# First 512 queries in four parts, the product of the decay factors in the lead-in, and the last combination in two steps

## The chip, the cores and the metric

The kernel runs on one core of one Trainium2 chip. The time is that of one execution on the device, in microseconds (us); several runs are made and their median is given. A core has five engines that each work through their own queue of instructions in order: TensorE (PE in the profile, with its weight loads as PEld), VectorE (DVE), ScalarE (ACT), GpSimd (POOL) and SyncE (SP, which here only starts transfers). They wait for one another by semaphores. Transfers between the chip's memory (HBM) and the on-chip buffer (SBUF) are made by 16 DMA engines. Results of TensorE land in PSUM, eight banks of 128 x 512 numbers.

## The reference

Two layers are computed on x of 2 sequences of 1024 tokens, 256 numbers each. Layer 0 is an attention with 16 query heads and 8 key heads of 16 numbers, whose output gates a feed-forward network with weights looked up from 16 values. Layer 1 is a recurrence whose output gates a mixture of 8 experts (two per token) with shared experts. Cut to what matters:

```python
# layer 0, attention
scores = jnp.einsum('bsdkg,btdk->bkgst', q, k) / jnp.sqrt(jnp.float32(E))
w = jax.nn.softmax(scores, axis=-1)
ctx = jnp.einsum('bkgst,btdk->bkgsd', w, v)          # then ctx @ W_O.T
# layer 0, feed-forward: w = lut[idx] for each of three weight matrices
h = jax.nn.silu(gate) * up
# layer 1, recurrence over t, for each head of 64 numbers
w = sigmoid(xn @ Wx @ Ww + bw)
state = (1.0 - w_t)[..., :, None] * state + k_t[..., :, None] * v_t[..., None, :]
y_t = jnp.einsum('bhi,bhij->bhj', r_t, state)        # then y @ Wout
# layer 1, experts
out = jax.nn.silu(g_sh) * u_sh @ shared_down.T
out = out + jnp.einsum('neh,ne->nh', y, combine)     # two experts per token
```

Each half of a layer is normalized first, and the feed-forward result goes through a SiLU, is multiplied by the attention's (or recurrence's) result and added to x.

## The kernel before

**The order.** All work is cut into steps. A step is a Python function that issues a few instructions on several engines, and has a letter. The string ORDER (lines 78 to 100, 1962 letters) says in which order the steps are issued; `go` takes letter after letter and calls that letter's next step. Nothing is reordered later: an engine gets its instructions in the order of the letters. So a step that waits on one engine holds up all later steps' instructions on that engine.

**The attention.** Tokens lie in 16 tiles of 128. For each tile there are statistics (`a`), a normalized copy (`b`), transposes for a pair of tiles (`e`), the product with the q, k, v weights (`f`, 4 TensorE passes of 512 columns; VectorE multiplies by cosine and sine, L205), the rotation on GpSimd (`g`, L223 and L226), and the transposes of the keys of a pair of tiles (`h`). `j` and `l` (`turn_q`, L264) transpose the queries of half a sequence, 512 queries of four heads, once without and once with their row maxima. A group g is four heads of a sequence; it has 16 units. `m` (`largest`, L274) makes for 128 queries and 512 keys of one head the scores and their maximum on VectorE (L290); four heads use four groups of 32 rows of TensorE. With the maximum as 17th number of a query, `w` (`weigh`, L296) makes scores of 128 keys and 512 queries that have the maximum taken off (L303), and ScalarE takes the exponential (L307). `v` (`gather`, L310) multiplies the four heads' exponentials by the values, adding up over the eight key tiles in one bank (L318). The first `l` needs the maxima of all 512 queries of its group, 32 `m` steps. `y`, `p` and `q` divide, transpose and project. Meanwhile GpSimd decodes the feed-forward weights (`z`, L252 and L256), up to 491 us. The exponentials have 22 buffers (EB).

**The middle.** `A` are the steps of layer 0's feed-forward: `gate_up0` (L506, L488) and `down0` (L522). At `>` the attention's pools are closed. Then eight loads for layer 1 are issued on SyncE, each of which waits until the memory that it takes is free: w1, gb, bw, gate, msk, wds, wgs (L581 to L599) and last `fold` (L1005), which is Wx transposed beside Ww, 512 KB, held in the buffer of `rd`. `rec_setup` (L1010, the first `i`) multiplies the two (wxwp, L1019), so that the decay needs one product per token rather than two, copies the result to wxw and then clears `rd`. It stands behind the first letter after `>`, so that TensorE meets it after one `down0`. `n` normalizes for layer 1, `o` is the routing, `s` the shared experts' first part, `i` the inputs of the recurrence.

**The recurrence and the end.** The recurrence of a block of 512 tokens (`r`) has seven `level` steps (L1127; 32 TensorE passes, then on VectorE L1134, L1162 and L1168) with `fold_in` (`c`, L1173: levels 0 to 4 on VectorE, L1193, the last two on ScalarE), then transposes (`turn_k`), states, reads and two `result` steps, which write s_sb. F, X, G, H, D and S handle 39 tiles of routed tokens: indirect fetch, transposes, gate and up (L912), transposes, down (L937) and an indirect write of the rows to y_h. When all rows are written, `k` loads the two expert results of 128 tokens, `d` makes the shared experts' second part (L970), and `u` combines:

```python
for k in range(2):                                                    # L983
    nc.vector.scalar_tensor_tensor(g, yk[:, k, :], wts[:, k, t : t + 1], src, ALU.mult, ALU.add)
    src = g
nc.scalar.activation(g, g, AF.Silu)                                   # L988
nc.gpsimd.tensor_tensor(g, s_sb[:, t, :], g, ALU.mult)                # L989
nc.vector.tensor_tensor(g, g, xs[:, t, :], ALU.add)                   # L990
nc.sync.dma_start(out_d[ts(t, P), :], g)                              # L991
```

Of the kernel before, what the change touches and what calls it, by code (L numbers as in the profile page):

```python
# [18 lines left out]
P = 128  # L19
# [20 lines left out]
EB = 22  # L40
# [38 lines left out]
abzbaazbbeebabfgeffbggbfahegffbgbjfhggfmmmhghmmmmemmmjmzmzmmmmmmmmmmmmmfmzmmmmmzmfjzmmmmlmwwwwmm  # L79
mwwwmwzmmwzzwmwmwmzmwmwwwmmmwwwwmwmmmvwwmmvmwmwzzwmwvwmmmmwwvgzwwmmgmmmlavvmwmmmwzwbvvmwzmwmwmwm  # L80
wmwmwmwjbmwzwmmmzzwweyhwmmwmmwmvwmzmmvzwwmmfmwwmvwmwgmwwzmavwmmmmwwvvwmwlvazvwmmmmwwfmmwwwwmjzmm
mwwzmwwmwzwmmmwzwmwvmwgmmmwzwvmwmwmwwmwmwwmzmmmlyvwmmmvmwwmvwmzwmvbwzmmwvwzmmbwvwwmmwwmmhezwwmmj
mwwmbmmwwvwwmmvzmmwwwwmvmmwmwwwvmmmwwwlfyjwwbmzwvzmwzmwvwwzmmvmwwmvwwmmwmmwfmwwmeywwmmzzmwmwwwmz
mgwzzmmfmmmmzwmwvvwwmmzzwwvmmmwgwmvmwwmwmvwmmwvmmwgmlfwwwmzvwzwmmvwmwmzmmwwjywmmwwzmmwgwmmmzwzhw
mwwwmmzvwmwmwmmvvwwzwzmmmwvmwmwwmwvmmzwmjlvwzwzmwmmwvmwwwmmmzvhwwmwmzmwzzzzzwmmwmwwzmmwwmmwwmwmm
vwwzmwzmmvwzmwwmwmvwmmmwzwzwvylwwmmwmzvmmmwwwvmmmmwwwzvvzwmwzzmzmzwmwjmzwwmmwzwwywmwzwmwmmvmzzwm
zmppzjvzzmmzwwwwwvzmwwzwlvmwmmvwmwwmwvmmmwwwzmvvwmmwwmwzmqmmwwwwmmqwwmzmwmzzwmvmmwwvwwmmmmmvvmmm
wwzmpylwwmmwmvwmwwmmwvwzwwwwzmmzvwwwmmwzmvwmmmmwwwqpwmmwwmwzmzjwmmmmwmmpqmmwwvvwmmwjvmzwwmvpwwww
qzy<pzqlwzmwmvmwmwmwwvmwmmwmwvwmwmwmvmwmwmwmwqmwmwzwmwwmwmmwmmwmwpwmwmmwmvvwmmmwmmvwwwmvlywwzmvm
wwwmmwvmwmwwmAAmwwzmvmwwmvwwzmmmmwzmAyAmzmmmwwwmAjwmmwzwmmAwwmwmwmmlwwmvmwwwmmmvvmwwwwwwvmmmvwww  # L90
wmwvvwzmmmwmwzzvwwzmmwwmmjwmwmzmmwmvwwmwvwmmmAAwwwwvmwmmjvwmwmlwmwwmmvmmmmmmwvvmwwwAyAmmwmvwmwzw
wmmzwmmwwwwmmmwwmwwmwwmwyqwmmwmmwwvvmwmmmwwvwmzwwlvwmmmmwwvwmwvmwmmmwwvvmwmzwmwmwwmwwyzmmmwwmwmA
wwmmzmwzmvvwwwmmmwvmwmwzwwwvlwzwwzwvwwwwvwwwwvvwwwwwwwwAywwwwvvwwwAwwwwpvvvwwwwAwwwwqpAvvvqApypA
qpqAAAqpAqAApApqAAq>AinnAAniAAAinAoAAAsAAiAninAAiAoAAnoArrnnrsoAAAAinrinAoAocAcnrAAAAoAAoAiociA)
nriinnrcsnrsocsooirsoosocosooisooosooooscoooosooooroooiooooroiroooioooooooroo]rFrrrFXiXcFGXFGFrH
GXHciXDGDrFFHHXSicSGDXrFHFiGcXDSFSrcHDGDGXiXSHGFFHGDXSDFHSXFGHDFGXrHcXDGSFiFHrSScXDSGXHGFrDDXrSr
HGHFrXGFSDFrHXGXDHGDSrrFHGSDHFiXXSrDSFGXcDrSHGFFHiXDHcDGFXSSGXSDHGDHrHXGDFrHcScFGiFSrXFDXcDHFSGr
ScDXGHGXrHDHFcGSXSFrDHDSXGrSrGFXHSiFGFDSHrXDrrrDrHGXcDHGSXDFrSHSFXSGcDrHGDcXrHGcDSSrHDSSkkrkicrc
kcdduukukuukridkkurkurkudurkkukukdukdruuuu
# [3 lines left out]
def attention(nc, tc, st, b0, small, singles, xs, xnT, s_sb, wlut, ident, epst, wqkv_d, rope_d, lut_d, idx_d, wo_d):  # L103
# [169 lines left out]

    def largest(n, i):  # L274

        g, u = divmod(n, 16)
        b, T = divmod(g, NQT)
        c, half = divmod(u, 2)
        if (g, c) not in tops:
            tops[g, c] = att2.tile([P, 2, 4], F32, tag="top", name=f"top_{g}_{c}", bufs=4)  # L280
        at = slice(SLOT * i, SLOT * (i + 1))
        ps = bank(f"mx_{n}_{i}")
        nc.tensor.matmul(  # L283
            ps,
            qTs["qTa", g, c // BC][at, ts(c % BC, P)],
            kTs[b][at, T // 2, ts(half, 512)],
            start=True,
            stop=True,
        )
        nc.vector.tensor_reduce(tops[g, c][:, half, i : i + 1], ps, AX.X, ALU.max)  # L290
        done[g, c] = done.get((g, c), 0) + 1
        if done[g, c] == 8:
            top = tops.pop((g, c))
            nc.vector.tensor_tensor(qns[b][:, T, c, :, HD], top[:, 0, :], top[:, 1, :], ALU.max)

    def weigh(n, i):  # L296

        g, u = divmod(n, 16)
        b, T = divmod(g, NQT)
        h, c = divmod(u, 8)  # L300
        at = slice(SLOT * i, SLOT * (i + 1))
        ps = bank(f"sc_{n}_{i}")
        nc.tensor.matmul(  # L303
            ps, kTs[b][at, T // 2, ts(c, P)], qTs["qTb", g, h][at, :], start=True, stop=True
        )
        e = att2.tile([P, 512], F32, tag="e", name=f"e_{n}_{i}", bufs=EB)
        nc.scalar.activation(e, ps, AF.Exp, scale=1.0 / math.sqrt(E))  # L307
        es[n, i] = e

    def gather(n):  # L310

        g, u = divmod(n, 16)
        b, T = divmod(g, NQT)
        h, c = divmod(u, 8)
        if c == 0:
            cxs[g, h] = bank(f"cx_{g}_{h}")
        for i in range(4):
            nc.tensor.matmul(  # L318
                cxs[g, h][SLOT * i : SLOT * (i + 1), :],
                values(b, c, 4 * (T // 2) + i),  # L320
                es.pop((n, i)),
                start=(c == 0),
                stop=(c == CPB - 1),
            )
        if c == CPB - 1:
            ct = att2.tile([P, 512], F32, tag="ct", name=f"ct_{g}_{h}", bufs=1)
            nc.scalar.copy(ct, cxs.pop((g, h)))
            cts[g, h] = ct
# [36 lines left out]
    def each(f, *ranges):  # L365
# [10 lines left out]
        "l": each(turn_q, ["qTb"], range(GROUPS), range(2)),  # L376
# [11 lines left out]
def two_layer_kernel(  # L388
# [55 lines left out]
    s_sb = pers.tile([P, NTC, E], F32, name="s_sb")  # L444

# [112 lines left out]

    steps["<"] = [end_sequence0]
# [21 lines left out]
    nc.sync.dma_start(w1, w1_d)  # L581
    gb = moe.tile([P, 2, KC], F32, name="gb")
    nc.sync.dma_start(gb, gb_d)
    bw = moe.tile([P, KC], F32, name="bw")
    nc.sync.dma_start(bw, bw_d)
    gate = moe.tile([P, KC, SLOT], F32, name="gate")
    nc.sync.dma_start(gate, gate_d)
    msk = moe.tile([P, NLEV, HALF], I32, name="msk")
    nc.sync.dma_start(msk, msk_d)
    wds = moe.tile([P, NFS, E], F32, name="wds")  # L590
    nc.sync.dma_start(wds, wds_d)
# [7 lines left out]
    nc.sync.dma_start(wgs, wgs_d)  # L599
# [379 lines left out]
    def combine(t):  # L979

        yk, src = tiles.pop(("yk", t)), tiles.pop(("s", t))
        g = mt[0].tile([P, E], F32, tag="g", name=f"g1_{t}", bufs=3)
        for k in range(2):  # L983
            nc.vector.scalar_tensor_tensor(
                g, yk[:, k, :], wts[:, k, t : t + 1], src, ALU.mult, ALU.add
            )
            src = g
        nc.scalar.activation(g, g, AF.Silu)  # L988
        nc.gpsimd.tensor_tensor(g, s_sb[:, t, :], g, ALU.mult)  # L989
        nc.vector.tensor_tensor(g, g, xs[:, t, :], ALU.add)  # L990
        nc.sync.dma_start(out_d[ts(t, P), :], g)  # L991
# [7 lines left out]
    wxw = rec.tile([P, KC, E], F32, name="wxw")  # L999
# [3 lines left out]

    fold = rd.rearrange("p a r s -> p (a r s)").rearrange("p (k f d) -> p k f d", k=KC, d=E)
    nc.sync.dma_start(fold[:, :, 0:2, :], fold_d)  # L1005
# [4 lines left out]
    def rec_setup():  # L1010
# [4 lines left out]
        ps = bank1("wxwp")  # L1015
        psv = ps.rearrange("p (k d) -> p k d", k=KC)
        for kc in range(KC):
            for k in range(KC):
                nc.tensor.matmul(  # L1019
                    psv[:, kc, :],  # L1020
                    fold[:, k, 0, ts(kc, P)],
                    fold[:, k, 1, :],
                    start=(k == 0),
                    stop=(k == KC - 1),
                )
        nc.scalar.copy(wxw, psv)
# [282 lines left out]
    def each(f, *ranges):  # L1309
# [22 lines left out]
        "u": each(combine, range(NTC)),  # L1332
    }
# [126 lines left out]
```

## Time and profile before

| | us |
|---|---|
| median of 3 runs (1015.49 to 1016.59) | 1015.66 |
| the profiled execution | 1016.48 |
| its span, first to last instruction | 1014.7 |
| first product with the q, k, v weights starts (its weights land at 12.07) | 12.2 |
| first maximum on VectorE | 32.3 |
| first exponential | 57.4 |
| last exponential's scores | 543.6 |
| closing of the attention's pools, first load behind it | 577.8 |
| last indirect write issued | 953.2 |
| first and last instruction of the combinations on VectorE | 963.1, 1007.6 |

The mean granted TensorE clock over the span is 0.983 of full. The page's first part gives busy time, share of the span and number of instructions for each engine; in its second part the span is cut into 40 slices of 25 us, and each digit is the busy share of a slice in tenths. A float32 product of TensorE shows as two passes; "x12" in a chain or timeline counts passes. In the chain of waits, "issue" is time in which the engine waited for nothing that the profile shows. TensorE's passes are pipelined and their ends are modelled, so durations of single passes overlap.

### The profile page before, as it was taken

What the parts mean: (1) busy time and instruction counts of PE and PEld (TensorE: products, weight loads), DVE (VectorE), ACT (ScalarE), POOL (GpSimd) and SP (SyncE); (2) the same over time, 40 slices, a digit from 0 to 9 for tenths busy, and PEclk for the clock granted to TensorE, in tenths of its full rate; (3) what the DMA queues carried; (4) which work ended last, traced back from release to release, by engine and by line L of the source; (5) the groups of instructions that cost most, each with busy time, mean ns of one, the idle gap of its engine ahead of it and who ended that gap; (6) DMA issues with size and microseconds to landing.
All of it is one profiled execution on the core that took longest, in us unless ns stands there. A gap on an engine that the chain in (4) does not pass through costs nothing.

```text
span 1014.7 us, 16476 instructions
## 1 busy us (share of the span) xinstructions
PE 961.0 (95%) x6324; PEld 503.6 (50%) x6324; DVE 628.8 (62%) x1234; ACT 536.5 (53%) x1007; POOL 578.6 (57%) x475
## 2 busy tenths in 40 slices
PE   6999999999999999999999889999999998999882
PEld 3444333343433443334335454656476776677671
DVE  4889887877777686667620133578757433554753
ACT  3167756566665666677687235435324444453221
POOL 6999899999999999999301020202002453434121
PEclk9999999999999999999999979999999999999997
DMA  4000000000000000000000121015101121212133
GB/s 148 1 1 12 1 12 1 1 12 1 12 2 12 1 12 1 1 1 1 1 1 1 56 102 42 1 42 170 44 1 37 62 66 52 64 48 63 64 115 93
DMA packets 18086, 34.48 MB, mean 34 GB/s; under 512 B 2878, under 2 KB 11344, under 8 KB 17664
## 3 DMA queue, kind: packets, MB, share of 16 engines
q1 hardware_dynamic: 12855, 21.18, 6.6%
q0 software_dynamic: 3920, 10.74, 3.4%
q10 hardware_dynamic: 1232, 1.51, 0.4%
q8 instruction: 51, 0.84, 0.3%
q14 instruction: 28, 0.22, 0.1%
HBM read 22.01 MB, written 11.40 MB: 33 GB/s over the span
## 4 chain that ended last, share of the span: by engine, by line
PE 86%; DVE 4%; issue 4%; ACT 2%; POOL 1%; DMA 1%; another core or an unknown queue 1%; ACTq 0%; POOLq 0%; DVEq 0%
PE sc L303 15%; PE mx L283 14%; PE cx L318 12%; PE gu L506 6%; PE gue L912 4%; PE gus L676 4%; PE d L522 4%; PE dne L937 3%; PE qkv L200 3%; PE lev L1155 3%; PE so L360 1%; PE kp L1059 1%; DVE w L1193 1%; PE s L1278 1%; POOL g L989 1%
## 5 line engine op out<-in xcount | busy, mean ns | idle before, releaser
L290 DVE TENSOR_REDUCE top<-mx 128x1 f32<-128x512 f32 x512 | 324.5, 684 | 85.0 <-PE mx L283 57.3
L307 ACT ACTIVATE e<-sc 128x512 f32<-128x512 f32 x512 | 272.0, 604 | 125.0 <-PE sc L303 68.7
L283 PE MATMUL mx<-kT,qTa 32*128 32x512 f32 x1024 | 281.2, 627 | 0.5 <-DVE top L290 0.5
L303 PE MATMUL sc<-qTb,kT 32*128 32x512 f32 x1024 | 277.9, 624 | 0.8 <-ACT qTb L271 0.8
L252 POOL TENSOR_SCALAR pick<-idx,lut 128x544 f32<-128x544 int32 x120 | 252.4, 2103 | 11.2
L256 POOL TENSOR_TENSOR wlut<-wlut,pick 128x544 f32<-128x544 f32 x120 | 160.7, 1339 | 10.0
L303 PEld LDWEIGHTS sc<-qTb,kT 32*128 32x128 f32 x1024 | 98.2, 183 | 84.5 <-DVE top L290 28.0
L283 PEld LDWEIGHTS mx<-kT,qTa 32*128 32x128 f32 x1024 | 100.9, 183 | 77.2 <-DVE top L290 34.6
L318 PE MATMUL cx<-e,vpad 128*32 128x512 f32 x1024 | 131.6, 602 | 0.0
L889 POOL DMA_INDIRECT xg<-xn_h,who x39 | 38.9, 996 | 104.9 <-ACT s_sb L1285 69.7
L532 POOL TENSOR_TENSOR sgt<-s_sb,g 128x256 f32<-128x256 f32 x16 | 12.1, 756 | 141.2 <-ACT g L530 141.2
L950 POOL DMA_INDIRECT y_h<-ye,who x39 | 40.7, 1043 | 73.3 <-ACT ye L945 28.2
L506 PE MATMUL gu<-xnT,wlut 128*128 128x512 f32 x160 | 73.4, 597 | 0.0
L318 PEld LDWEIGHTS cx<-e,vpad 128*32 128x32 f32 x1024 | 22.6, 108 | 87.0 <-issue 75.3
L912 PE MATMUL gue<-wgu,xT 128*128 x156 | 53.3, 464 | 1.6 <-ACT hTe L930 0.8
L921 DVE TENSOR_TENSOR sge<-sge,gue 128x176 f32<-128x176 f32 x39 | 13.2, 337 | 59.8 <-ACT sge L920 55.3
L522 PE MATMUL d<-wlut,h 128*128 128x256 f32 x192 | 45.4, 389 | 1.1 <-DVE h L497 0.6
L506 PEld LDWEIGHTS gu<-xnT,wlut 128*128 128x128 f32 x160 | 29.1, 190 | 33.9 <-issue 28.1
L676 PE MATMUL gus<-xnT,wgs 128*128 128x512 f32 (+1 forms) x96 | 43.3, 597 | 0.0
L937 PE MATMUL dne<-wd,hTe 88*128 x156 | 40.8, 384 | 2.5 <-DVE w L1193 1.2
L516 DVE TENSOR_TENSOR h<-sg,gu 128x512 f32<-128x512 f32 x20 | 13.7, 687 | 46.0 <-ACT sg L515 24.6
L1162 DVE TENSOR_TENSOR rd<-rd,up 128x512 f32<-128x512 f32 x48 | 31.0, 687 | 17.6 <-PE xgTp L901 4.4
(219 smaller groups left out, 1283.9 us busy)
## 6 DMA issues: line engine op xcount, KB each, us to landing
xn_h<-xn SPq DMA_DIRECT2D x16, 256.0 KB, 2.7
yk<-y_h SPq DMA_DIRECT2D x16, 256.0 KB, 2.9
wgu<-in_wgu SPq DMA_DIRECT2D x1, 2816.0 KB, 11.3
idx<-in_idx SPq DMA_DIRECT2D x8, 272.0 KB, 2.8
out_x<-g SPq DMA_DIRECT2D x16, 128.0 KB, 1.7
wd<-in_wd SPq DMA_DIRECT2D x1, 1408.0 KB
w<-in_w SPq DMA_DIRECT2D x1, 1024.0 KB
wgs<-in_wgs SPq DMA_DIRECT2D x1, 704.0 KB, 6.2
```

The costliest lines, as they stand in the source:

```text
L252: nc.gpsimd.tensor_scalar(dst, codes[piece], float(j), lut[:, j : j + 1], ALU.is_equal, ALU.mult)
L256: nc.gpsimd.tensor_tensor(wlut[:, at], wlut[:, at], dst, ALU.add)
L283: nc.tensor.matmul(ps, qTs["qTa", g, c // BC][at, ts(c % BC, P)], kTs[b][at, T // 2, ts(half, 512)], start=True, stop=True,)
L290: nc.vector.tensor_reduce(tops[g, c][:, half, i : i + 1], ps, AX.X, ALU.max)
L303: nc.tensor.matmul(ps, kTs[b][at, T // 2, ts(c, P)], qTs["qTb", g, h][at, :], start=True, stop=True)
L307: nc.scalar.activation(e, ps, AF.Exp, scale=1.0 / math.sqrt(E))
L318: nc.tensor.matmul(cxs[g, h][SLOT * i : SLOT * (i + 1), :], values(b, c, 4 * (T // 2) + i), es.pop((n, i)), start=(c == 0), stop=(c == CPB ...
L506: nc.tensor.matmul(hT0[which], wlut[:, lo + kc * P :][:, 0:P], xnT[:, kc, ts(n, 512)], start=(kc == 0), stop=(kc == KC - 1),)
L522: nc.tensor.matmul(po[:, 0:E], hidden(n)[:, f, ts(k, P)], wd0[:, f, :], start=(f == 0), stop=(f == NF0 - 1),)
L676: nc.tensor.matmul(ps[:sz, which, :], wgs[:, kc, which * SH_CH + lo : which * SH_CH + lo + sz], xnT[:, kc, ts(n, 512)], start=(kc == 0), s ...
L912: nc.tensor.matmul(ps[:, 0 : 2 * EI], xT[:, kc, :], late["gu"][:, kc, bass.ds(e * (2 * EI), 2 * EI)], start=(kc == 0), stop=(kc == KC - 1),)
L937: nc.tensor.matmul(ps[:, 0:E], hT[:, k, :], late["d"][:, k, bass.ds(e * E, E)], start=(k == 0), stop=(k == 1),)
```

## The change

The kernel gets a new ORDER of 1982 letters with two new letters, `W` (once) and `U` (16 times), and three more `l`.

- **Queries in parts.** The first transposes of 512 queries with their maxima become four `turn_first` steps of 128 queries. For the first eight units a `weigh` makes four products of 128 queries by 128 keys side by side in a bank, for one part of the queries and four key tiles; `gather` takes them in 16 products of 128 columns. The first `l` now stands behind 14 `m`, before behind 36. By the 64th `m` both orders have 32 `w` and 4 `v`. Before the first `m` the new order has 9 `f`, 5 `e`, 3 `h` and 1 `j`; the old one 8, 4, 2 and 1. EB is 21; the most exponentials that the new order has open is 21, the old one 22.
- **Decay product.** `fold` is loaded on ScalarE's queue, behind the attention's first loads, into the first part of s_sb. The product is the step `W`, behind the first `l`. The other seven loads stay behind `>`, in another order. `rec_setup` keeps its other instructions, behind two `n` now. `>` stands behind 27 `A` rather than 26: the first `down0` of the second block is now issued ahead of it, directly behind the last `gate_up0` of that block and ahead of the last `project`.
- **Last combination.** `u` ends with the SiLU; the product on GpSimd, the addition (VectorE for even tiles, GpSimd for odd ones) and the write are `U`. At the last `S` the new order has issued 46 `r` and 22 `c`, the old one 49 and 25; at `]`, where the routing ends, 17 `r` against 13.

The two ends of the order and the code:

```diff
-EB = 22
+EB = 21
...
-abzbaazbbeebabfgeffbggbfahegffbgbjfhggfmmmhghmmmmemmmjmzmzmmmmmmmmmmmmmfmzmmmmmzmfjzmmmmlmwwwwmm
...
-ScDXGHGXrHDHFcGSXSFrDHDSXGrSrGFXHSiFGFDSHrXDrrrDrHGXcDHGSXDFrSHSFXSGcDrHGDcXrHGcDSSrHDSSkkrkicrc
-kcdduukukuukridkkurkurkudurkkukukdukdruuuu
+aaabbbabeazbebfgefgfgbzbbbfgehfgeffghgfjfhmmgmhmmgmmmmmmjfmmmlWmwmzmmwwwmmwlmmwmmwzmwwmwmmzwmmwm
...
+DHXrcSHDGXDGHFFXGHXSGDFXSrHcDFHGGSFXSXFrSDDHGSHDGSFSXDHrrHiGXSDDrFGXHrrSSrDrHSGDrHcDSSckrdkkuukU
+ukrdkUkucUurciUkkiuUUkurckduUrcdcurUkukUkuUrrUdukurUkrduUUuuUU
...
+    def turn_first(c):
+        if c == 0:
+            qTs["qTb", 0, 0] = att2.tile([P, 512], F32, tag="qTb", name="qTb_0_0")
+        ps = bank(f"qTbp_0_{c}_0")
+        nc.tensor.transpose(ps[:, 0:P], qns[0][:, 0, c], ident)
+        nc.scalar.copy(qTs["qTb", 0, 0][:, ts(c, P)], ps[:, 0:P])
...
     def weigh(n, i):
...
+        if n < 8:
+            for k in range(4):
+                nc.tensor.matmul(
+                    ps[:, ts(k, P)],
+                    kTs[0][at, 0, ts(c % 2 * 4 + k, P)],
+                    qTs["qTb", 0, 0][at, ts(c // 2, P)],
+                    start=True,
+                    stop=True,
+                )
+        else:
...
     def gather(n):
...
+        if n < 8:
+            for k in range(4):
+                for i in range(4):
+                    nc.tensor.matmul(
+                        cxs[0, 0][SLOT * i : SLOT * (i + 1), ts(c // 2, P)],
+                        values(0, c % 2 * 4 + k, i),
+                        es[n, i][:, ts(k, P)],
+                        start=(c % 2 == 0 and k == 0),
+                        stop=(c % 2 == 1 and k == 3),
+                    )
...
-        "l": each(turn_q, ["qTb"], range(GROUPS), range(2)),
+        "l": each(turn_first, range(BC)) + each(turn_q, ["qTb"], range(GROUPS), range(2))[1:],
...
+    wxw = pers.tile([P, KC, E], F32, name="wxw")
...
+    fold = s_sb.rearrange("p c e -> p (c e)")[:, 0 : 2 * KC * E].rearrange(
+        "p (k f d) -> p k f d", k=KC, d=E
+    )
+    nc.scalar.dma_start(fold, fold_d)
+    def weights_of_decays():
+        ps = bank1("wxwp")
...
+        nc.scalar.copy(wxw, psv)
+    steps["W"] = [weights_of_decays]
...
     def combine(t):
...
-        g = mt[0].tile([P, E], F32, tag="g", name=f"g1_{t}", bufs=3)
+        g = mt[0].tile([P, E], F32, tag="g", name=f"g1_{t}", bufs=4)
...
         nc.scalar.activation(g, g, AF.Silu)
+        tiles["g", t] = g
+    def finish(t):
+        g = tiles.pop(("g", t))
         nc.gpsimd.tensor_tensor(g, s_sb[:, t, :], g, ALU.mult)
-        nc.vector.tensor_tensor(g, g, xs[:, t, :], ALU.add)
+        add = (nc.vector, nc.gpsimd)[t % 2]
+        add.tensor_tensor(g, g, xs[:, t, :], ALU.add)
         nc.sync.dma_start(out_d[ts(t, P), :], g)
...
-    fold = rd.rearrange("p a r s -> p (a r s)").rearrange("p (k f d) -> p k f d", k=KC, d=E)
-    nc.sync.dma_start(fold[:, :, 0:2, :], fold_d)
+    loads = [(bw, bw_d), (gb, gb_d), (gate, gate_d), (w1, w1_d)]
+    for to, src in loads + [(wgs, wgs_d), (msk, msk_d), (wds, wds_d)]:
+        nc.sync.dma_start(to, src)
...
     def rec_setup():
...
-        ps = bank1("wxwp")
...
-        nc.scalar.copy(wxw, psv)
         nc.gpsimd.memset(rd, 0.0)
...
+        "U": each(finish, range(NTC)),
```

## The prediction

> **What bounds it now.** I read the page's busy rows and 40 slices first, then the chain of waits, then the timelines of the three places that the change touches.
>
> ```profile
> PE 961.0 (95%) x6324; PEld 503.6 (50%) x6324; DVE 628.8 (62%) x1234; ACT 536.5 (53%) x1007; POOL 578.6 (57%) x475
> PE   6999999999999999999999889999999998999882
> DVE  4889887877777686667620133578757433554753
> ```
>
> TensorE is the bound, except in three places. In the first slices VectorE is nearly full. Slice 23 has a dip. In the last two slices TensorE falls to 8 and 2 while work goes on. Between these places a microsecond taken from TensorE is a microsecond of the span, so I price each place by what it keeps TensorE from.
>
> The dip, in the chain from 575 to 600 us (start, duration, what), then the same stretch by windows (the columns after the window: PE, PEld, DVE, ACT, POOL busy, granted clock):
>
> ```profile
> 578.30 2.83 PE d L522 x12
> 581.13 7.23 issue
> 588.36 3.75 PE wxwp L1019 x8
> 592.11 6.18 PE d L522 x24
> ```
>
> ```profile
> 581.00:588.40 7.40, 0.17 (x2) 0.07 (x1) 2.25 (x10) 0.39 (x1) 1.45 (x2) 0.69 0.85 315
> 588.40:594.00 5.60, 5.60 (x13) 4.47 (x14) 0.00 (x0) 1.84 (x2) 1.81 (x1) 0.50 0.01 3
> ```
>
> TensorE stands 7.23 us for `fold`, the eighth of eight loads that SyncE issues from 577.8 on (DMA share 0.85). Then it runs at half clock until 594.
>
> The end, by the timeline of one period:
>
> ```profile
> 999.66 0.47 DVE L984 SCALAR_TENSOR_TENSOR g<-yk,wts,ds 128x256 f32<-128x256 f32 x1
> 1000.17 0.48 DVE L984 SCALAR_TENSOR_TENSOR g<-yk,wts,g 128x256 f32<-128x256 f32 x1
> 1000.69 0.42 ACT L988 ACTIVATE g<-g 128x256 f32<-128x256 f32 x1 [2.21 <-DVE g L984]
> 1001.19 0.72 POOL L989 TENSOR_TENSOR g<-s_sb,g 128x256 f32<-128x256 f32 x1 [1.90 <-ACT g L988]
> 1001.94 0.43 DVE L990 TENSOR_TENSOR g<-g,xs 128x256 f32<-128x256 f32 x1 [1.29 <-POOL g L989]
> 1002.29 0.47 DVE L984 SCALAR_TENSOR_TENSOR g<-yk,wts,ds 128x256 f32<-128x256 f32 x1
> ```
>
> Each tile goes round VectorE, ScalarE, GpSimd and VectorE again, 2.63 us, and the next cannot start, since the add of L990 stands ahead of it in VectorE's queue. Sixteen periods are 42 us. The last add ends at 1007.6; the 7.1 us from there to 1014.7 (output write, end) I leave.
>
> **The change, part by part.** The sum is made against the profiled execution, 1016.48 us (span 1014.7).
>
> *The dip.* 7.23 us of standing, 3.75 us of wxwp, and the half clock on the 24 `d` passes that follow (6.18 against 2 x 2.59 us for warm ones): 1.0. Together 12.0. What is late next: the new order has three `down0` tiles (2.6 us each) before the first thing that needs a load (`logits`: gate), and the loads start at about 580, so 8 us cover 3. Given back: the first `down0` now follows directly on `gt`, with no `project` between, and waits for its SiLU and product, 0 to 1.3 us; I take 1. **-11.0** (-12 to -8).
>
> *wxwp in the lead-in.* Eight passes of 256 columns; the nearest row is `ds`, 24 passes in 5.4 us, so 1.8 us of TensorE, and one ScalarE copy of 0.59, at a time when VectorE is the bound (24.05 of 25 us busy in 31-56). Without that cover: 1.8 us. Its load, 512 KB, is issued on ScalarE's queue behind wqkv and rope. One issue is 0.53 us, and ScalarE's first statistic (table load at 4.03) is behind it: I charge 0.5 us. Wqkv, which lets the first product start (12.07), is ahead of it in the same queue; the first codes (GpSimd's wait, 13.29) may land up to 1.9 us later (512 KB at the 280 GB/s of the first 10 us). GpSimd's decode has 30 us in hand (done at 491, the last weights used from 523).
>
> *Four parts of 128.* The first score no longer waits for 32 maxima but for 8. Yet by the 64th maximum the new order has done the same 32 scores and 4 gathers as the old one, so the gain is only what VectorE stood in between: 0.95 + 0.72 + 2.99 us in 31-56, 56-70 and 70-89. Against it, one more `qkv` (1.72), `turn_x` (0.66) and `turn_k` (0.60) come before the first maximum: 3.0 us later, of which 0.96 returns, since that `cs` is not in the way later. The passes grow from 64 to 256 for scores and for gathers. The nearest rows:
>
> ```profile
> L1113 PE MATMUL dia<-rT,kT 64*128 64x128 f32 x128 | 8.2, 278 | 0.0
> L651 PE MATMUL logits<-xnT,gate 128*32 128x128 f32 x64 | 2.6, 279 | 0.0
> ```
>
> `dia` runs 32 passes of 128 columns in 1.99 us on two row groups: one pass per 0.124 us and group, weight load included. Eight passes for a (chunk, head) are then 1.0 us on its group, against two passes of 512 columns now (0.43 us each, 0.86). `logits` (column groups as in `gather`) runs 16 passes in 0.64 us, so a unit of 32 is 1.28 against 1.06 now. Extra: 32 x 0.14 / 4 + 8 x 0.22 = 2.9 us if the four groups run side by side. TensorE has about 10 us to spare there: in 31-89 its rows add up to some 48 of 58 us (171 maximum and 81 score passes at 0.125, 64 gather passes at 0.12, qkv and transposes 9). [...] The row shows 0.124 with the load in it, so I take the row[...]. Between none recovered with passes dearer (+6) and all recovered (-3) I take **+1.0**, near the row, with the 0.5 us of issue in it.
>
> *Order before the last spread.* Three `level` steps of the last block (2 to 4) and three `fold_in` (1 to 3) move behind it. TensorE loses 3 x 1.15 = 3.5 us before it. There VectorE was fuller (930-955: TensorE 21.6, VectorE 20.1 of 25 us), and 3 x 2.15 + 2.63 + 1.46 + 1.44 = 12 us leave it, so up to the 3.4 us that TensorE stood may go too. **-5.5** (-3.5 to -6.9).
>
> *The tail.* Counted from the end of the last `dne` (952.24) to the last add (1007.62), the old one takes 55.4 us. The new one, in VectorE's order: rest of fold 0 (2.4), folds 1 to 4 (2.63 + 1.46 + 1.44 + 1.47), levels 2 to 6 at 2.15 (10.6), eight combinations at 1.02 (8.2) and four adds at 0.43 (1.7): 30 us back to back; the first combination, which needs the gathered rows (some 7 us after that `dne`), finds them ready. Then the chain from level 6 to the last result: transposes 1.0, copy 1.2, `add` 1.1, states 1.6, reads 1.9, `ds` 2.6, `s` 1.9 + 1.9, `ds` 2.6, with waits 16.2. Then tile 15: 1.0 + 0.42 + 0.72 + 0.72 on GpSimd and gaps, 3.1. Sum 49.3. EB 21 holds the most that the new order has open (21); the g buffers (4) hold the two tiles that `u` runs ahead of `U`.
>
> But so far GpSimd worked only while VectorE waited; now they overlap. [...] The trace of before has such a pair:
>
> ```profile
> L294 DVE TENSOR_TENSOR qn<-top x64: 166/334/1359, 37.9 to 515.0; 128x4 f32<-128x4 f32 x64
> ```
>
> It reads two SBUF tiles, 4 numbers a lane, beside GpSimd's decode: 166 ns at best, 1359 at worst. At 65.14 us it took 1.11 and ended when a GpSimd addition did. [...] By the row (mean 466, so 0.30 of waiting where GpSimd is always busy), for the 13 that fall in the first 30 us: 13 x 0.30 = 4; later VectorE has time. I take the row: 53.4, **-2.0** (-6 to +11).
>
> Sum: 1.0 - 11.0 - 5.5 - 2.0 = -17.5, so 999.0. The median of the runs is 0.8 below the profiled one: **998.2**.
>
> **Rivals.** (1) *The overlap is free.* The tail takes 49.3 (-6), VectorE's standing is recovered (-2.5), with -12 and -6.5: -27, 988.7. For: the operations are short and can slip between each other. Against: L294. (2) [...] 1 - 11 - 5.5 + 11.3 = -4.2, 1011.5. For: of 30 us of VectorE, 16 have two SBUF inputs. Against: the mean of L294. (3) *Slower: small passes in a row.* In a piece-wise score eight passes stand on one row group before the next letter names another. If TensorE cannot run past them, 512 passes of 0.112 (`dia` at its steady pace) are 57 us against 17 now: +40, less 10 to spare, +30 in place of +1: 1028. It decides from 0.088 us per pass ((17 + 10 + 18.5)/512) on. For: now only two passes stand on a group. Against: `logits` and `dia`, at 0.040 and 0.062. (4) *No change*, with losses elsewhere in the new order that eat the gain: 1015.7.
>
> **How the numbers follow.** Forecast 0.49, (1) 0.24, (2) 0.16, (3) 0.07, (4) 0.04. A change under 0.2% (2 us) can't be told from none. Faster: 0.49 + 0.24 + 0.15 = 0.88; same 0.03; slower 0.07 + 0.02 = 0.09. The range, 986 to 1008, holds the forecast and (1); it leaves out most of (2), and (3) and (4).
>
> **What would show it.** Dip: no standing over 1.5 us near 580, no half clock there; wxwp near 40 us at 1.8. Lead-in: first maximum near 36, and the 64th no later than before. Tail: periods of VectorE near 1.3 to 2 us, products at L989's successor over 0.73 us or adds over 0.43 [...]. I am wrong if the middle (600 to 930) has new gaps in TensorE, since I carry it over unchanged, or if score passes take over 0.088 us.

## The result and the profile after

The changed kernel takes 1001.86 us (median of 4 runs, 1000.27 to 1002.63); beside it the kernel before takes 1015.58 (4 runs, 1013.9 to 1016.59). The ratio is 0.9864, with a 95% interval of 0.9846 to 0.9883: 13.7 us faster. The profiled execution is the fastest of the four, 1000.27 us with a span of 998.5, so the two traces differ by 16.2 us. The forecast was 998.2, in a range of 986 to 1008.

From the page of the changed kernel, the busy row of TensorE and its and VectorE's 40 slices:

```profile
PE 955.1 (96%) x6708; PEld 519.1 (52%) x6708; DVE 631.1 (63%) x1226; ACT 533.6 (53%) x1007; POOL 587.9 (59%) x483
PE   5999999999999999999999999999999999989875
DVE  4899887877878667576750143867856525531893
```

The 8s in TensorE's slices 23 and 24 are gone; the dip before the change lay across both. The end has changed its look: VectorE is at 8 and 9 in slices 38 and 39, where it was at 7 and 5, and TensorE is still at 5 in the last slice, where it was at 2. The chain of waits around the old dip (start, duration, what):

```profile
572.96 1.72 PE gt L521 x4
574.68 2.59 PE d L555 x12
...
578.60 8.04 PE d L555 x36
586.64 0.87 PE x1Tp L494 x8
587.51 12.02 PE gu L539 x28
```

The 7.23 us of "issue" and wxwp are no longer in it, and twelve `d` passes take 2.59 to 2.68 us, at a granted clock of 1.00 from 575 to 595. The loads still take their time (DMA share 0.96 in 585 to 590), but nothing waits for them.

For the sum, the two traces are cut at three places at which both orders have issued the same work, or nearly so: a `qkv` near 102 us, the first transposed gathered rows (`xgTp`; 17 `r` are issued by then in both) and the end of the last `dne`.

| us | before | after | difference | predicted |
|---|---|---|---|---|
| `qkv` near 102 us | 102.31 | 102.02 | -0.3 | +1.0 |
| from there to the first `xgTp` | 668.15 | 653.52 | -14.6 | -11.0 |
| from there to the end of the last `dne` | 181.78 | 181.49 | -0.3 | -5.5 |
| from there to the last addition | 55.38 | 53.94 | -1.4 | -2.0 |
| from there to the end of the span | 7.1 | 7.5 | +0.4 | 0 |

Two terms do not fit, and they nearly cancel: more is won ahead of the gathered rows than the dip was thought to hold, and nothing between them and the last spread.

### The profile page after: what moved, and what is told of

It reads as the page before. It is cut to its first block, busy times and chain, and to the rows that moved or that the text cites. A ratio compares the mean times of both kernels' runs of the same rounds, so it can differ in the third digit from the quotient of the medians.

```text
span 998.5 us, 17239 instructions
## 1 busy us (share of the span) xinstructions
PE 955.1 (96%) x6708; PEld 519.1 (52%) x6708; DVE 631.1 (63%) x1226; ACT 533.6 (53%) x1007; POOL 587.9 (59%) x483
## 4 chain that ended last, share of the span: by engine, by line
PE 88%; DVE 7%; ACT 2%; issue 1%; POOL 0%; DMA 0%; another core or an unknown queue 0%; POOLq 0%; ACTq 0%; SPq 0%; DVEq 0%
PE sc L322 14%; PE mx L291 14%; PE cx L350 12%; PE gu L539 7%; PE gue L959 4%; PE gus L723 4%; PE d L555 4%; PE dne L984 3%; PE qkv L200 3%; PE lev L1194 2%; DVE top L298 2%; PE so L392 2%; DVE w L1232 1%; DVE rd L1201 1%; PE sc L314 1%; PE s L1317 1%
## 5 line engine op out<-in xcount | busy, mean ns | idle before, releaser
L291 PE MATMUL mx<-kT,qTa 32*128 32x512 f32 x1024 | 279.6, 625 | 0.1
L322 PE MATMUL sc<-qTb,kT 32*128 32x512 f32 x960 | 258.5, 625 | 0.0
L291 PEld LDWEIGHTS mx<-kT,qTa 32*128 32x128 f32 x1024 | 102.0, 183 | 66.3 <-DVE top L298 27.1
L322 PEld LDWEIGHTS sc<-qTb,kT 32*128 32x128 f32 x960 | 90.0, 183 | 80.1 <-DVE top L298 28.5
L350 PE MATMUL cx<-e,vpad 128*32 128x512 f32 x960 | 123.5, 602 | 0.0
L936 POOL DMA_INDIRECT xg<-xn_h,who x39 | 39.2, 1005 | 116.2 <-ACT s_sb L1324 71.4
L549 DVE TENSOR_TENSOR h<-sg,gu 128x512 f32<-128x512 f32 x20 | 13.8, 688 | 70.9 <-ACT sg L548 54.8
L968 DVE TENSOR_TENSOR sge<-sge,gue 128x176 f32<-128x176 f32 x39 | 12.8, 337 | 60.3 <-ACT sge L967 57.3
L1201 DVE TENSOR_TENSOR rd<-rd,up 128x512 f32<-128x512 f32 x48 | 33.1, 731 | 28.2 <-PE lev L1194 10.1
L539 PEld LDWEIGHTS gu<-xnT,wlut 128*128 128x128 f32 x160 | 29.0, 190 | 33.7 <-issue 29.5
```

What stands on the lines that cost most here:

```text
L291: nc.tensor.matmul(ps, qTs["qTa", g, c // BC][at, ts(c % BC, P)], kTs[b][at, T // 2, ts(half, 512)], start=True, stop=True,)
L322: nc.tensor.matmul(ps, kTs[b][at, T // 2, ts(c, P)], qTs["qTb", g, h][at, :], start=True, stop=True)
L350: nc.tensor.matmul(cxs[g, h][SLOT * i : SLOT * (i + 1), :], values(b, c, 4 * (T // 2) + i), es.pop((n, i)), start=(c == 0), stop=(c == CPB ...
L539: nc.tensor.matmul(hT0[which], wlut[:, lo + kc * P :][:, 0:P], xnT[:, kc, ts(n, 512)], start=(kc == 0), stop=(kc == KC - 1),)
```

## The experiments

The runs fell on several chips. The kernel before takes 1003.9 and 1004.8 us on two of them and 1014.4 to 1015.6 on the others, so kernels are compared by their ratio to the kernel before on the same chip, and traces from chip to chip only between the marks above. A "tail" is the time from the end of the last `dne` to the last addition.

**Each part alone, and the old end (one chip, the kernel before at 1004.83).**

`e1_load_early`, the kernel before with the early load (one `w` moved behind a `v`, so that 21 exponentials are enough):

```diff
-EB = 22
+EB = 21
...
-mmmmlmwwww
+mmmmlWmwwww
...
+    nc.scalar.dma_start(fold, fold_d)
...
+    steps["W"] = [weights_of_decays]
...
-    fold = rd.rearrange("p a r s -> p (a r s)").rearrange("p (k f d) -> p k f d", k=KC, d=E)
-    nc.sync.dma_start(fold[:, :, 0:2, :], fold_d)
+    loads = [(bw, bw_d), (gb, gb_d), (gate, gate_d), (w1, w1_d)]
+    for to, src in loads + [(wgs, wgs_d), (msk, msk_d), (wds, wds_d)]:
+        nc.sync.dma_start(to, src)
```

> The kernel before with one part of the change alone: the 512 KB of fold on ScalarE's queue in the lead-in, wxwp after the first turned queries, the seven other loads in the new order. Theory (the dip was worth its whole 12.0 us: 7.23 standing, 3.75 wxwp, 1.0 half clock; the lead-in pays at most 1 us for the issue): 1004 us (1003 to 1005.5), no standing over 1.5 us near 580, the d passes at 2.59 us for twelve at once. Rival (the standing only changes its name: gate or wgs arrive late, or the first down products wait for their SiLU): gain of 8 at most, 1008 or more, with a new wait of 3 us or more between 580 and 620.

Measured: 994.46 us, ratio 0.9898 (0.9882 to 0.9914), 10.4 us faster. From the `gt` near 575 us to the first `xgTp` it takes 182.5 us, the kernel before 194.2 (in the trace `b2_before`) to 195.5: 11.7 to 13.0 for the dip. But the `qkv` near 102 us comes at 104.69 instead of 102.31, more than the 0.5 us charged. All of that is lost by the first maximum (34.65 instead of 32.27), so it is the load and not wxwp: `fold` is issued at 7.40, and ScalarE's first own instruction, behind it in the queue, starts at 7.76 instead of 4.03. From the first maximum to that `qkv` both traces take 70.04 us, one with wxwp between and one without. The theory holds, and the rival's new wait is not there.

`e2_parts`, the kernel before with `turn_first` and the two branches `if n < 8`, and the first 201 letters of the new order without `W`:

> The kernel before with the four parts of 128 alone: lead-in letters of the changed order without wxwp up to the point (some 200 letters in, about 95 us) where both orders have done the same work, then the order of before. Theory (pieces are free, lead-in even): 1015.2 us (1014.2 to 1016.2), first maximum some 1.2 us earlier than in the changed kernel, since ScalarE's queue has one load less. Rival 1 (the prediction's term, pieces dearer and first maximum 3 us later): 1016.6. Rival 2 (the parts take away VectorE's standing in the lead-in and carry it to the end): 1012.5 or less.

Measured: 1004.65 us, ratio 1.0021 (1.0002 to 1.0040), and something that no theory had: of 22 runs, 14 took 1002.4 to 1004.8 at a mean clock of 0.984 to 0.987 and 8 took 1010.6 to 1015.7 at 0.973 to 0.979. The profiled one is of the eight. Its `qkv` near 102 us comes at 108.80. Behind a wait of TensorE of 0.70 us for the first turned queries the granted clock is 0.50 from 44.2 to 64.7, with TensorE busy by its records (a line of the timeline, then windows: length, TensorE busy, clock, DMA share, GB/s):

```profile
42.08 0.82 PE L314 MATMUL sc<-qTb,kT 32*128 32x128 f32 x5 [0.70 <-ACT qTb L280]
```

```profile
44.00:48.00 4.00, 4.00 (x31) 0.53 0.00 0
48.00:52.00 4.00, 4.00 (x29) 0.50 0.00 0
```

The median of the 14 is 1003.9, so without that the parts are even, as the theory says. `e9_late_load` takes this up.

`e3_old_end`, the changed kernel with the order of before behind the first gathered rows, and a combination in one step again:

```diff
-        tiles["g", t] = g
-
-    def finish(t):
-        g = tiles.pop(("g", t))
         nc.gpsimd.tensor_tensor(g, s_sb[:, t, :], g, ALU.mult)
-        add = (nc.vector, nc.gpsimd)[t % 2]
-        add.tensor_tensor(g, g, xs[:, t, :], ALU.add)
+        nc.vector.tensor_tensor(g, g, xs[:, t, :], ALU.add)
```

> The changed kernel with the end of the kernel before: from the first gathered rows on (behind the end of the routing) the old order, combination of a chunk in one step on VectorE's add. What it loses against the changed kernel is what the new end is worth. Theory (by the traces 14.9 of the 16.2 us are won by the first gathered rows, so the end brings little): 1003.5 us (1002.5 to 1005). Rival (the prediction's terms, 5.5 before the last spread and 2.0 behind it): 1009.4.

Measured: 990.07 us, ratio 0.9852 (0.9836 to 0.9869). `e4_new_end`, the reverse: the kernel before up to the first gathered rows, then the new order with `finish`:

> The kernel before with the new end alone: old order and late load of fold up to the first gathered rows, then the new order with the combination in two steps. Theory: 1014.2 us (1013 to 1015.2). Rival (the prediction's 7.5 us): 1008.1. The dip near 580 stays as it was in both.

Measured: 1001.38 us, ratio 0.9964 (0.9952 to 0.9977): 3.5 us faster. Neither value fell on a theory. By `e4_new_end` the new end is worth more than the 1.4 us of the trace and less than the 7.5 of the prediction; by the ratio of `e3_old_end`, against 0.9864 for the changed kernel on another chip, it is worth nothing. So old and new end had to stand side by side on one chip.

**The end, GpSimd beside VectorE and another order (a second chip, the kernel before at 1003.89).**

> The changed kernel as it is, beside the others on one chip. On the chip of the last four runs the kernel before takes 1004.8 us, not 1015.6, and TensorE has no gaps between 780 and 900 us there. Theory A (the change's gain is what the single parts gave on that chip: load 10.3, end 3.5, parts nothing): ratio 0.986, 13.8 us less than before. Theory B (the new end is worth nothing once the rest is new, as e3_old_end at 0.9852 suggests): ratio 0.985 to 0.986 as well, but then the next kernel does not differ from it.

Measured: 986.90 us, ratio 0.9835 (0.9821 to 0.9848), 17.0 us faster here, more than the 13.8 that the single parts add up to.

> The changed kernel with the old end once more (the same kernel as e3_old_end), now beside the changed kernel on one chip. Theory A (end worth 3.5 us, as e4_new_end showed on the kernel before): 3.5 us slower than the changed kernel. Theory B (worth nothing behind the new order): within 1 us of it. The prediction's terms (5.5 and 2.0): 7.5 us slower.

Measured: 990.72 us, ratio 0.9870 (0.9855 to 0.9885): 3.8 us slower than the changed kernel, so theory A. The traces tell where: the last `dne` ends at 926.98 with the old end and at 922.43 with the new one (4.6), the tail from there to the last addition takes 54.6 and 55.0. All of the gain lies ahead of the last spread, and on this chip the two-step combination does no more than pay for the steps that were moved behind it.

Why was that 4.6 us not there in the first comparison? The window from 765 to 905 us of the kernel before and of the changed kernel, both on the chip of the result, and then of the changed kernel on this one (length; PE, PEld, DVE, ACT, POOL busy; clock; DMA share; GB/s):

```profile
765.00:905.00 140.00, 133.23 (x1035) 94.85 (x1034) 69.93 (x128) 64.31 (x153) 60.66 (x59) 0.99 0.18 57
```

```profile
765.00:905.00 140.00, 131.23 (x987) 94.00 (x986) 61.57 (x120) 61.95 (x159) 63.24 (x63) 0.99 0.19 59
```

```profile
765.00:905.00 140.00, 139.10 (x1115) 102.80 (x1114) 64.23 (x130) 66.43 (x169) 68.91 (x67) 1.00 0.21 63
```

On the chip of the result TensorE stands 6.8 us among the gathered tiles before and 8.8 after, on this one 0.9. From the first `xgTp` to the last `dne` the old order takes 181.8 and 180.4 us on chips where the kernel before takes 1014 to 1016 us, and 171.1 to 171.2 on those where it takes 1004 to 1005. The new order takes 180.5 to 181.6 on chips of the first kind, in four traces, and 166.2 to 166.7 on those of the second. So the moved steps shorten this stretch on the chips where TensorE is full in it (139.1 of 140 us busy on this one), and not where it stands.

`e6_less_gpsimd` measures what GpSimd's operations cost VectorE's. It leaves out GpSimd's product for the first eleven tiles and five of its eight additions, so these tiles' output lacks that work; VectorE's instructions stay:

```diff
-        nc.gpsimd.tensor_tensor(g, s_sb[:, t, :], g, ALU.mult)
+        if t >= 11:
+            nc.gpsimd.tensor_tensor(g, s_sb[:, t, :], g, ALU.mult)
         add = (nc.vector, nc.gpsimd)[t % 2]
-        add.tensor_tensor(g, g, xs[:, t, :], ALU.add)
+        if t >= 11 or t % 2 == 0:
+            add.tensor_tensor(g, g, xs[:, t, :], ALU.add)
```

> The changed kernel, whose tail leaves out GpSimd's product and addition for the first eleven tiles, so their output lacks the product with the attention result; VectorE's instructions and their order are unchanged. Theory [...]: the pairs of rd return from 1.82 to 1.29 us, additions from 0.95 to 0.43, level 6 ends some 4.5 us earlier after the last dne, and the kernel is 4 to 5 us faster than the changed one. Rival (the stretched instructions meet the writes and reads of DMA in that time): the pairs stay at 1.82, the kernel gains less than 1 us.

Measured: 982.50 us, ratio 0.9780 (0.9767 to 0.9794), 4.4 us less than the changed kernel. Level 6 ends 29.5 us after the last `dne` instead of 34.7; the tail takes 51.3 instead of 55.0. Two of VectorE's groups of lines in the tail, changed kernel first (busy, mean ns; idle before):

```profile
L1232 DVE COPY_PREDICATED w<-msk,lev 64x512 f32<-64x512 int32 x10 | 9.4, 942 | 0.1
L1201 DVE TENSOR_TENSOR rd<-rd,up 128x512 f32<-128x512 f32 x10 | 8.5, 895 | 0.0
```

```profile
L1234 DVE COPY_PREDICATED w<-msk,lev 64x512 f32<-64x512 int32 x10 | 9.4, 944 | 0.1
L1203 DVE TENSOR_TENSOR rd<-rd,up 128x512 f32<-128x512 f32 x10 | 6.4, 683 | 0.0
```

The ten `rd` products, with both inputs in SBUF, fall from 895 to 683 ns. The ten copies to `w`, one of whose inputs TensorE wrote to PSUM, keep their 0.94 us. The reads and writes of the tail are issued in both kernels, and the pair of this run at 949.58 takes 1.29 us with an output write issued in it, at 950.04; so the rival falls. The theory's numbers came: pairs at 1.28 to 1.29, additions at 0.42 to 0.43 up to 957 us. By what means GpSimd slows VectorE is not shown. Per pair with one product in it the loss is 0.54 us; the row of before (L294) had given 0.30 per operation. How two overlaps look in the timeline of the changed kernel, in the trace of the result:

```profile
942.69 1.28 DVE L1201 TENSOR_TENSOR rd<-rd,up 128x512 f32<-128x512 f32 x2
...
949.03 1.82 DVE L1201 TENSOR_TENSOR rd<-rd,up 128x512 f32<-128x512 f32 x2
...
949.51 0.79 POOL L1040 TENSOR_TENSOR g<-s_sb,g 128x256 f32<-128x256 f32 x1 [0.85 <-ACT g L1035]
...
962.68 1.81 DVE L1201 TENSOR_TENSOR rd<-rd,up 128x512 f32<-128x512 f32 x2
962.69 1.25 POOL L1040 TENSOR_TENSOR g<-s_sb,g 128x256 f32<-128x256 f32 x1
```

With GpSimd idle a pair takes 1.28 us. With one GpSimd product in it, it takes 0.54 more, while the product takes 0.79 beside 0.72 to 0.73 alone: here it is VectorE that loses. In the last overlap, where both start together, the product takes 1.25: there GpSimd loses too.

`e7_levels_first` was meant to beat both ends. Until level 6 VectorE does levels, `fold_in` and combinations in turn, and behind it stands idle while TensorE works. So the combinations go behind it:

```diff
-ckrdkkuukUukrdkUkucUurciUkkiuUUkurckduUrcdcurUkukUkuUrrUdukurUkrduUUuuUU
+ckrkdkcrikcricrcukdrcdrukukUukrUrukUukUdukUukUdrukUukUdukUukUdruUuUuUuUUU
...
-        "d": [lambda: down_s(0, 0, BC), lambda: down_s(1, 0, BC)]
-        + [lambda n=n, k=k: down_s(n, k, 2) for n in (2, 3) for k in (0, 2)],
+        "d": [lambda: down_s(0, 0, BC)]
+        + [lambda n=n, k=k: down_s(n, k, 2) for n in (1, 2, 3) for k in (0, 2)],
```

> The changed kernel with another order behind the last spread: levels 2 to 6 of the last block first, one combination between them, the other fifteen behind level 6 while TensorE computes states, reads and results; the down products of block 1 in two halves, so that a large bank is free for the transposes. Worked out from the rows: level 6 ends 21 to 24 us after the last dne (33.7 now), TensorE's remaining work ends at 41 to 44, the last addition at 45 to 47 instead of 53.9. Theory (order of VectorE's queue is what the tail waits for): 7 to 9 us faster than the changed kernel. Rival 1 ([...] fifteen combinations now run in 20 us with 24 GpSimd instructions beside them): 3 to 5 us faster. Rival 2 (down products now stand in the way of the last results on TensorE): within 2 us of the changed kernel.

Measured: 987.22 us, ratio 0.9832 (0.9819 to 0.9846): no gain. Level 6 ended 21.9 us after the last `dne`, as worked out, but the last addition came 56.1 us after it, later than the 55.0 of the changed kernel. The idle column of VectorE's first combining instruction names what came in between:

```profile
L1031 DVE SCALAR_TENSOR_TENSOR g<-yk,wts,ds 128x256 f32<-128x256 f32 x16 | 7.6, 478 | 10.9 <-DMA out_x<-g 10.7
```

**The waits behind level 6, and the load put back (a third chip, the kernel before at 1014.94).**

> The kernel before as it is, for a trace from the chip of the experiments, where it takes 1004 us and not 1015.6. Theory (the difference between the chips lies where gathered rows arrive, since the runs so far have no gaps of TensorE between 780 and 900 us there): the same times as in the first trace to within 1 us up to 770, dip included, and some 10 us less from 770 to the last dne. Rival (another clock or other loads): the difference is already there at 600.

Measured: 1014.34 us, ratio 0.9995 (0.9984 to 1.0006), a chip like that of the result, so the theory was not put to the test as meant. Its trace serves as the kernel before for the marks.

`e8_rows_early` reads ten of the row pairs ahead, into weights that are dead by then, and has an order of its own behind the last spread:

```diff
-        y = mt[0].tile([P, 2, E], F32, tag="yk", name=f"yk_{t}", bufs=4)
+        if t < 10:
+            y = late["gu"][:, t // 5, ts(t % 5, 2 * E)].rearrange("p (k e) -> p k e", k=2)
+        else:
+            y = mt[0].tile([P, 2, E], F32, tag="yk", name=f"yk_{t}", bufs=4)
```

> The kernel e7_levels_first, with ten of the sixteen gathered row pairs read into the dead gate weights of the experts, so that fourteen reads can start without waiting for a combination. In e7 level 6 ended 21.9 us after the last dne, as worked out, but VectorE then stood 1 to 2 us before nearly every combination for the rows (four buffers, a read of some 4 us behind each). Theory (those waits are the whole of what was lost): VectorE runs on behind level 6, the last addition comes 45 to 47 us after the last dne (55.0 in the changed kernel), 978 us, 8 to 9 us faster than the changed kernel. Rival 1 ([...] 24 GpSimd instructions now meet VectorE's, at up to 0.5 each): 3 to 5 us faster. Rival 2 (TensorE's down products, or the queue of writes at the end): within 2 us of e7.

Measured: 998.77 us, ratio 0.9852 (0.9834 to 0.9870), tail 51.4. Half of the waits remained (5.9 us), and their name shows that the expectation had misread the row above: `out_x<-g` is the output write. A combination waits for the result buffer `g` of the tile four before, and that is free only when its write has landed. The rows had a part in that: in `e7_levels_first` SyncE took 18.33 us, from 928.46 on, to issue seven reads, with the output writes behind them in the same queue; here ten reads took 5.02. Since the order changed too, the two are not told apart.

`e9_late_load`, the changed kernel with the load and wxwp where they were before the change:

> The changed kernel with fold loaded last and wxwp behind the first phase again, as before the change, everything else new. Theory A (parts add up: e1 gave 10.3 on the kernel before): 10 to 12 us slower than the changed kernel, 997.5. Theory B (wxwp in the lead-in also keeps TensorE busy at 41 us, where the kernel with the parts alone fell to half clock for some 20 us in a third of its runs): besides that, some of the runs lie 6 to 9 us higher, with a granted clock lower by 0.01. Without that effect the runs stay within 3 us of each other.

Measured: 1025.61 us (six runs, 1022.6 to 1026.4), ratio 1.0105 (1.0088 to 1.0123): 10.7 us slower than the kernel before, and some 24 slower than the changed one by its ratio, twice what theory A gives. Against `e8_rows_early`, whose trace is from the same chip and whose order is the same up to the tail but for `W`, 8 us are lost by 111 us (`qkv` at 110.92 instead of 103.02; 7.2 of them behind the first maximum) and 14.8 between `gt` and the first `xgTp`. The second is the dip, deeper than before the change, since the chain to the loads now runs through a GpSimd product, which ends at 587.2; before, the loads started at 577.8:

```profile
586.48 0.73 POOL sgt L564
...
589.84 6.66 DMA wgs<-in_wgs
596.49 1.51 issue
598.00 3.75 PE wxwp L1056 x8
```

The first is theory B, but in every run, as it seems: the six lie within 4 us of each other. TensorE's windows in the lead-in (length, busy, clock, DMA share, GB/s), this kernel first, then the changed one in its trace of the second chip:

```profile
44.00:48.00 4.00, 3.29 (x25) 0.70 0.01 2
48.00:52.00 4.00, 4.00 (x29) 0.50 0.00 0
52.00:56.00 4.00, 4.00 (x27) 0.50 0.00 0
56.00:60.00 4.00, 4.00 (x34) 0.50 0.01 4
60.00:64.00 4.00, 4.00 (x46) 0.67 0.00 0
```

```profile
44.00:48.00 4.00, 4.00 (x53) 1.00 0.01 2
48.00:52.00 4.00, 3.95 (x50) 1.00 0.02 4
```

And what stands at the start of it, in the timelines of the two:

```profile
44.94 0.89 PE L314 MATMUL sc<-qTb,kT 32*128 32x128 f32 x5 [0.71 <-ACT qTb L280]
```

```profile
41.90 0.33 PE L279 MATMUL qTbp<-cst,qn 128*128 128x128 f32 x1
42.06 1.99 PE L603 MATMUL wxwp<-s_sb 128*128 128x256 f32 x8
```

The first turned queries go through ScalarE before a score can use them. Without wxwp TensorE stands 0.71 us for that copy, and then runs some 17 us at half clock. With wxwp the pause is filled: the granted clock is 1.00 from 40 to 68 us in the traces of the changed kernel on both chips, of `e3_old_end` and of `e8_rows_early`.

That the pause is the cause is not shown. The kernel before stands as long for the same copy (0.77 us, up to 56.18), and the clock is 1.00 behind it; 3.4 us at half clock come earlier, up to 47.9, with TensorE busy by its records:

```profile
40.00:50.00 10.00, 10.00 (x36) 0.83 0.00 0
50.00:60.00 10.00, 9.23 (x50) 1.00 0.00 1
```

```profile
56.18 1.14 PE L303 MATMUL sc<-qTb,kT 32*128 32x512 f32 x8 [0.77 <-ACT qTb L271]
```

In `b2_before`, the same kernel, the clock is 0.91 from 40 to 60 us, which is 3.6 us at half clock; in `e4_new_end`, with the same lead-in, it is 0.97 up to 50 and 1.00 from 50 to 100. So what goes with the long stretches is the pause together with the small pieces behind it. No run takes these two apart, and with both 14 of the 22 runs of `e2_parts` took 1002.4 to 1004.8 us.

**A version that beats both (a fourth chip, the kernel before at 1014.38).** `e10_more_buffers` puts all row pairs into the dead weights, ten places in turn, and uses the room for result buffers, again with an order of its own behind the last spread:

```diff
+        at = t % 10
+        y = late["gu"][:, at // 5, ts(at % 5, 2 * E)].rearrange("p (k e) -> p k e", k=2)
...
-        g = mt[0].tile([P, E], F32, tag="g", name=f"g1_{t}", bufs=4)
+        g = mt[0].tile([P, E], F32, tag="g", name=f"g1_{t}", bufs=12)
```

> The kernel e8_rows_early with all sixteen row pairs read into the dead gate weights (ten places in turn) and, in the room that this frees, twelve result buffers in place of four. In e8 the last addition came 51.4 us after the last dne (55.0 in the changed kernel on its chip), and VectorE still stood 5.9 us for output writes, since a combination needs the buffer of the tile four before. Theory (those waits are what is left over the 45 to 47 us worked out): 46 us (45 to 47.5) from the last dne to the last addition, ratio to the kernel before 0.977 to 0.980 against 0.9852 for e8, and no wait for an output write on VectorE. Rival 1 ([...] more GpSimd instructions beside VectorE's): 49 to 50 us, ratio 0.983. Rival 2 (TensorE's down products, which end 41 us after the last dne in e8, decide): 48 us, with VectorE standing for ds.

Measured: 993.64 us, ratio 0.9799 (0.9784 to 0.9813), against 0.9864 (0.9846 to 0.9883) for the changed kernel on a chip of the same pace. The tail takes 49.1 us. No wait for an output write is left; what is left are longer additions beside GpSimd, and the waits for its products:

```profile
L1032 DVE SCALAR_TENSOR_TENSOR g<-wgu,wts,ds 128x256 f32<-128x256 f32 x16 | 7.6, 472 | 0.0
...
L1043 DVE TENSOR_TENSOR g<-g,xs 128x256 f32<-128x256 f32 x8 | 7.0, 878 | 3.8 <-POOL g L1041 3.8
```

Eight additions take 0.88 us in place of 0.43, and wait 3.8 us for the products. So by the tail's length rival 1 is right, and the ratio is at the slow end of the theory's range.

## Why the prediction was nearly right

- **The dip, -11.0.** Right in kind and size: `e1_load_early` won 11.7 to 13.0 there. What the step did not see is that wxwp goes with a whole clock in its new place: without it both traces of the four parts show a long stretch at half clock (20.5 us in `e2_parts`, 17.1 in `e9_late_load`). Taken out of the new kernel, the move is worth some 23 us (`e9_late_load`), not 12: 14.8 at the dip, which is deeper in the new order, and 8 in the lead-in.
- **wxwp in the lead-in.** It took 1.99 us at 41.3 us, as said (1.8, near 40). ScalarE's first instruction came 1.15 us later than before, not 0.5, and 3.7 later in the one trace with the old lead-in: the term that was too small is the issue of the load, not wxwp. In the new lead-in the lateness was made good by the 64th maximum; in the old one, 2.4 us were not.
- **The four parts, +1.0.** Measured between -0.3 (the chip of the result) and +1.2, with the first maximum 2.3 us later (3.0 said) and the lateness gone by the 64th (77.79 against 78.14). By the order itself the new kernel has 30 `w` behind its 64th `m` and 32 only behind the 65th, which costs nothing that the traces show. A unit of gathers in pieces takes 1.08 us beside 1.06 for a whole one. Score pieces in a row on one row group start 0.112 us apart, weight load included: the row `dia` (0.124) gave the right answer. That is above the 0.088 that was named as a sign of being wrong and from which rival 3 was to decide, but rival 3's picture was wrong: passes of `largest` start in between (L291 at 44.01 and 44.23 between those of L314 at 43.90, 44.12 and 44.30), and the lead-in is even.
- **Order before the last spread, -5.5.** This is the step that failed. It took "3 x 1.15 = 3.5 us" off TensorE and hoped for TensorE's standing besides. On the two chips where the kernel before takes 1004 to 1005 us the stretch is shorter by 4.6 and 5.0 us, inside the step's own -3.5 to -6.9. On the chip of the result it is shorter by 0.3: there TensorE has 2.0 us less to do in 765 to 905 and stands 2.0 us longer. The trace of before showed such gaps (133.23 of 140 us busy in that window), and the step treated the stretch as bound by TensorE.
- **What was carried over.** The middle was taken as unchanged. The -14.6 us between the marks hold some 12 for the dip; the other 2.6 come from the new order ahead of the gathered rows, which no step priced (from the `qkv` to the first `xgTp` the early load alone takes 655.2 us, and with the new order 652.7 to 653.6). That it made good half of the failed step is luck, and with it the nearness of the sum.
- **The tail, -2.0.** Measured -1.4 (53.94 us; 53.4 said) on the chip of the result, but +0.4 on the second. The overlap with GpSimd was put at 4 us; leaving out two thirds of GpSimd's operations ended level 6 5.2 us earlier and made the tail 3.6 shorter. Level 6 came 33.7 us after the last `dne`, where 30 and the 4 for the overlap give 34; the chain from there to the last down product took 16.1 (16.2 said), and the last tile 4.1 (3.1 said); products of 0.97 to 1.25 us and additions of 0.93 to 0.97 were the signs named. Rival 1 would have had a tail of 49.3. Rival 2 had all 24 GpSimd operations (16 products, 8 additions, at the 0.725 us of L989) on top of it: 66.7, 11.3 more than before. That each costs its whole time was the author's estimate; the overlaps above cost a pair 0.54 us.
- **The median.** Profiled executions differ by 16.2 us, medians by 13.7. The execution of before lay 0.9 above its median, the one of after 1.6 below: the 0.8 taken off was the right way for one trace and not for both.

What stays open: what sets the long half clock of the four parts without wxwp, and why TensorE stands among the gathered tiles on some chips. The clock is the same (0.99 to 1.00 in that window), and the changed kernel's passes there differ little between the two chips: 476 and 465 ns for gate and up, 392 and 380 for down, 229 on both for the levels. The time from a gather's issue to its landing, 2.9 us on the second chip, is not resolved in the trace of the first. Nor was it tried whether any other TensorE work at 41 us goes with a whole clock as wxwp does.

## What to carry to other kernels

Price a step that is moved at its new place too: work put into a gap of a starved engine may go with a whole clock behind it, so that two edits of one change can be worth more together than the sum of each alone (here some 23 us for the move of load and product, not 12). Before a saving on the busiest engine is counted, look whether that engine is full in that very stretch; where it already stands, less work for it can be more standing. Behind a pipeline that is taken apart, count the buffers whose release is a DMA write: in `e7_levels_first` level 6 came 12.8 us earlier than in the changed kernel on the same chip, and waits of 10.7 us for output writes helped to cost all of it.

## What the runs showed of the hardware

- A pause of TensorE of 0.70 us (`e2_parts`) and of 0.71 us (`e9_late_load`), in a phase in which its products use 32 rows of the array, was followed by 20.5 and 17.1 us at a granted clock of 0.50, while its records show it busy without a gap. The kernel before shows two such stretches: 3.4 us near 46, with TensorE busy, and 10.2 us from 583.8 to 594.0, in and behind the stand of 7.23 us. The four lengths lie near 1, 3, 5 and 6 times the shortest. With the parts alone the long stretch came in 8 of 22 runs by their times and clocks; in the changed kernel without wxwp the six runs lie together, at the level of the profiled one, which has it.
- In the changed kernel a pair of VectorE operations with two SBUF inputs took 0.5 us longer with one GpSimd product in it (1.82 against 1.28), and the product 0.76 to 1.25 us instead of 0.73; without two thirds of GpSimd's operations the ten operations took 683 ns each instead of 895, and the ten copies with one input in PSUM 944 instead of 942. The tail was 3.6 us shorter.
- The same program, the kernel before, takes 1004 us on two chips and 1014 to 1016 on three, with a mean granted clock of 0.983 to 0.987 on the first and of 0.981 to 0.987 on the others. For the changed kernel, traced on one of each, the spans differ by 13.6 us and the stretch of gathers and scattered writes by 14.8.
